# Layer 0's results in DRAM by quarter, line and position, in a two-layer scan of convolutions

## The chip, the cores and the metric

The kernel runs on one core of one Trainium2 chip. The metric is the device time of one execution in microseconds (us), as a median of several runs. A profile is one further execution with the hardware profiler on; its span runs from the first to the last instruction.

## What is computed

The input x is 32 images of 48 channels, 64 rows (H) and 128 columns (W), float32. There are two layers. Each one normalizes its input over groups of channels, runs four scans over it, and adds the result to its input:

```
def step(w, b):
    def f(carry, inp):
        nxt = inp + _conv1d(carry, w, b)        # 5 taps along the line, 48 -> 48 channels
        return (nxt, nxt)
D = scan(down) over h = 1..63;   U = scan(down's weights) over h = 62..0
R = scan(right) over w = 1..127; L = scan(left) over w = 126..0

x = x + _L0_conv_ref(_gn(x), L0 weights)
x = x + _L1_conv_ref(_gn(x), L1 weights)
```

Each line of a scan (a row of 128 positions, or a column of 64) needs the line before it. A row scan of one group of images is 2 x 63 = 126 steps, a column scan 2 x 127 = 254.

## The kernel before

**Work and order.** The 32 images are four groups of 8. Rows are scanned a group at a time, columns a pair of groups at a time, so there are twelve phases, in the fixed order of `PHASES` (L103): rows of layer 0 groups 0 and 1, columns of layer 0 pair 0, rows of layer 0 group 2, rows of layer 1 group 0, rows of layer 0 group 3, columns of layer 0 pair 1, rows of layer 1 groups 1, 2 and 3, columns of layer 1 pairs 0 and 1. They are counted from 0 here, so phase 3 is the rows of layer 0 group 2, phase 7 the rows of layer 1 group 1, phases 10 and 11 the columns of layer 1. That makes 8 x 126 + 4 x 254 = 2024 steps, each of nine matmuls (L856) and three DVE additions out of PSUM (L865), in one chain.

**Tiles.** Eight positions of a line times 48 channels are 384 lines of partitions, that is three tiles (`o` = 0, 1, 2) of 128 partitions. Position `e` (0 to 7) takes the partitions that `PIECES` (L50) gives: 48 channels at a stretch, two of the positions cut in two, so that a tile consists of three or four pieces of 48, 32 or 16 partitions. In a row phase the free axis of a tile runs over h, and over 16 blocks of 8 positions with 8 images each. In a column phase it is turned round: partitions are h modulo 8 and channel, and the free axis goes over w.

**The transposition is in DRAM.** All tensors between phases lie in DRAM: `xin` (the input, reordered), `ups` (`upa`, `upb`: the results of the row scans) and `mid` (layer 0's results, which are layer 1's input). A column phase works on quarters of W (`j` = 0 to 3) in three slots of the arena. A quarter is 2 groups x 3 tiles = 6 units; a unit is 128 partitions x 2048 elements, 1.05 MB. `mid` before is `kept("mid")` (L188): for each group 48 channels, each with 65,536 elements in the order of `by_col` (L243), and a pad.

**Who uses mid.**
- `keep_result` (L790) writes a unit of layer 0's column phases (2 and 6) to `mid`, in pieces of 48, 32 or 16 partitions, each partition one run of 8 KB. It is issued on SP's queue, four steps after `add_residual` (L785, POOL) has added the layer's input to the unit.
- `move_rows` (L657) loads rows for a row phase, in the same pieces; each run is 128 bytes. For layer 1 (phases 4, 7, 8, 9) it reads `mid` through `by_row` (L220), 8 rows a DMA, on SP's queue. `scale_rows` (L680, ACT) normalizes 16 rows in 24 ACTIVATEs after that.
- `load_residual` (L776) loads the unit that is added to a result. In layer 1 (phases 10 and 11) it reads `mid` by `by_col`, in pieces, on ACT's queue; in layer 0 it reads `xin` on SP's.

**The order of the work** is written out: `at(t, fn, ...)` puts a piece of work at step t of the whole chain, and `in_order` (L255) fixes the order of the instructions on every engine and queue as they are traced, so that a queue's next DMA is never issued before the one ahead of it. All DMAs are recorded under L249. The DMAs of SP and ACT take eight semaphores in turn, so that one waits until the DMA eight places before it has landed. `plan_rows` (L968) loads rows 16 at a time (`LOAD`): after a column phase at steps -28, -12, 4 and 20 of the phase, scaled at -13, 3, 19 and 35; otherwise at -54, -43, 0 and 11, scaled at -22, -8, 16 and 30. `plan_cols` (L1011) adds the results of quarters 3, 2, 1, 0, 32 steps from one to the next, a unit each 4.5 steps (7 in quarter 0 ahead of a row phase). In layer 1 a result is then brought into the output's order (`permute_unit`, L806, line L813) and stored (`store_result`, L821, runs of 128 bytes), or held in DRAM (`hold_result`) and sent out later (`let_result`, L834). The last quarter of the last phase is added by DVE after the last step (`last_results`, L1105).

**Statistics.** `scaling` (L352) turns means and variances into scale and offset for a group. In its short form (`if not slack`, L394), used for three groups of x, a variance is spread over partitions by three small matmuls (`expand`, L371), DVE adds a constant, ACT takes the square root (L405), and then the mean is spread (L406).

Of the kernel before, what the change touches and what calls it, by code (L numbers as in the profile page):

```python
# [29 lines left out]
F32 = mybir.dt.float32  # L30
# [3 lines left out]
C = 48  # L34
# [8 lines left out]
E8 = 8  # L43
FULL = 128
NG = E8 * C // FULL
NQ = 4
# [73 lines left out]
def kernel(  # L120
# [67 lines left out]
    def kept(name):  # L188

        return [  # L190
            dram.tile([C, CHANNEL + PAD], F32, tag=f"{name}{g}", name=f"{name}{g}")[:, 0:CHANNEL]
            for g in range(NGRP)
        ]
# [3 lines left out]
            dram.tile([E8 * NQ, C, UNIT], F32, tag=f"xin{g}", name=f"xin{g}")  # L197
            for g in range(NGRP)
        ],
        kept("mid"),  # L200
    ]
    ups = [kept("upa"), kept("upb")]
    taps = [
# [28 lines left out]
    def x_by_col(t, e, j):  # L232


        return t[e * NQ + j]

    def x_put(t, r):

# [4 lines left out]
    def by_col(t, e, j):  # L243


        return t.rearrange("c (i q n) -> i q c n", i=E8, q=NQ)[e, j]

    def dma(dst, src, queue=None):
        (queue or nc.sync).dma_start(dst, src)  # L249
# [34 lines left out]
    def pieces(o):  # L284
        return [(e, c0, c1, p0) for e, c0, c1, g, p0 in PIECES if g == o]
# [66 lines left out]
    def scaling(key, layer, g, averages, masks, slack=0):  # L352


        n = len(masks)
        yield from averages(key, slack)
        mean_p, var_p = averages.result
        pool = nc.gpsimd

        def average(ps, *terms):  # L360
            for k, rhs in enumerate(terms):
                for i in range(n):
                    nc.tensor.matmul(
                        ps,
                        masks[i],
                        rhs[:, i],
                        start=k == 0 and i == 0,
                        stop=k == len(terms) - 1 and i == n - 1,
                    )

        def expand(ps, *terms):  # L371
            for o in range(NG):
                for k, rhs in enumerate(terms):
                    nc.tensor.matmul(
                        ps[:, o], maskp[:, o], rhs, start=k == 0, stop=k == len(terms) - 1
                    )

        def small(name):
            return stat_tile([FULL, NG, GB], name, key)

        ps = ps_stat.tile([FULL, 2 * NG + 2, GB], F32, tag="ps_stat", name=f"ps_{key}")
        average(ps[:, 0], mean_p)
        yield
        scale, offset = (
            stat_pool.tile(
                [FULL, NG, GB], F32, tag=f"{t}{layer}{g}", name=f"{t}{layer}{g}"
            )
            for t in ("scale", "offset")
        )
        coeffs[layer, g] = scale, offset  # L390
        mean, var = ps[:, 1 : 1 + NG], ps[:, 2 + NG :]
        spare = small("dev")
        dev = spare[:, 0:n]
        if not slack:  # L394
            far = ps[:, 1 + NG : 2 + NG]
            nc.vector.tensor_tensor(far, mean_p, ps[:, 0:1], ALU.subtract)
            nc.vector.tensor_tensor(dev, mean_p, ps[:, 0:1], ALU.subtract)
            nc.vector.tensor_tensor(far, far, dev, ALU.mult)
            nc.vector.tensor_tensor(dev, far, var_p, ALU.add)
            yield  # L400
            expand(var, dev[:, 0])
            yield
            nc.vector.tensor_scalar(var, var, GN_EPS, None, ALU.add)
            r0 = small("std")
            nc.scalar.activation(r0, var, AF.Sqrt)  # L405
            expand(mean, mean_p[:, 0])  # L406
            yield
            yield
            nc.vector.reciprocal(r0, r0)
            nc.vector.tensor_tensor(var, var, r0, ALU.mult)  # L410
            nc.vector.tensor_tensor(var, var, r0, ALU.mult)
            nc.vector.tensor_scalar(var, var, -0.5, 1.5, ALU.mult, ALU.add)
            nc.vector.tensor_tensor(scale, var, r0, ALU.mult)
            nc.vector.tensor_tensor(offset, mean, scale, ALU.mult)
            nc.vector.tensor_scalar(offset, offset, -1.0, None, ALU.mult)
            return
        mean_s = small("mean")
        if n > 1:
            mean_c = stat_tile([FULL, GB], "mean_c", key)
            nc.vector.tensor_copy(mean_c, ps[:, 0])  # L420
            yield
            expand(mean, mean_c)
            yield
            nc.vector.tensor_tensor(dev, mean_p, mean, ALU.subtract)
            nc.vector.tensor_copy(mean_s, mean)
        else:
            nc.vector.tensor_tensor(dev, mean_p, ps[:, 0:1], ALU.subtract)
        pool.tensor_tensor(dev, dev, dev, ALU.mult)
        if n == 1:
            pool.tensor_tensor(dev, dev, var_p, ALU.add)  # L430
        yield
        for _ in range(slack):
            yield
        if n == 1:
            expand(var, dev[:, 0])
        else:
            average(ps[:, 1 + NG], dev, var_p)
            yield
            var_c = stat_tile([FULL, GB], "var_c", key)
            nc.vector.tensor_copy(var_c, ps[:, 1 + NG])  # L440
            yield
            expand(var, var_c)
        yield
        var_s = small("var")
        nc.vector.tensor_scalar(var_s, var, GN_EPS, None, ALU.add)
        std = small("std")
        nc.scalar.activation(std, var_s, AF.Sqrt)
        if n == 1:
            expand(mean, mean_p[:, 0])
        yield  # L450
        if n == 1:
            nc.vector.tensor_copy(mean_s, mean)
        yield
        for _ in range(slack):
            yield
        r0 = std
        nc.vector.reciprocal(r0, std)
        t0 = spare
        pool.tensor_tensor(t0, var_s, r0, ALU.mult)
        pool.tensor_tensor(t0, t0, r0, ALU.mult)  # L460
        yield
        pool.tensor_scalar(t0, t0, -0.5, 1.5, ALU.mult, ALU.add)
        pool.tensor_tensor(scale, r0, t0, ALU.mult)
        pool.tensor_tensor(offset, mean_s, scale, ALU.mult)
        pool.tensor_scalar(offset, offset, -1.0, None, ALU.mult)
# [185 lines left out]
    def row_views(k):  # L651
        return [slot[i].rearrange("p (o h n) -> p o h n", o=NG, h=HALF) for i in slots(k)]
# [4 lines left out]
    def move_rows(k, h0, h1, to_dram, q=None):  # L657

        _, layer, g = PHASES[k]
        view = row_views(k)[h0 // HALF]  # L660
        t = (ups if to_dram else source)[layer][g]
        for h in range(h0, h1, E8):
            end = min(h1, h + E8)
            for o in range(NG):
                for e, c0, c1, p0 in pieces(o):
                    here = view[p0 : p0 + c1 - c0, o, h % HALF : h % HALF + end - h]
                    if to_dram or layer:
                        there = by_row(t, e, h, end, q)[c0:c1]
                    else:
                        there = x_by_row(t, e, h, end)[c0:c1]  # L670
                    if q is None:
                        here = here.rearrange("p h (q n) -> p (h q) n", q=NQ)
                    else:
                        here = here[:, :, q * RUN : (q + 1) * RUN]
                    if to_dram:
                        dma(there, here)
                    else:
                        dma(here, there)

    def scale_rows(k, h0, h1):  # L680
        _, layer, g = PHASES[k]
# [36 lines left out]
    def quarter(k, j):  # L718
        return slot[slots(k)[j % 3]].rearrange("p (o s n) -> p s o n", s=2, o=NG)
# [56 lines left out]
    def load_residual(k, j, i, nat):  # L776
        _, layer, pair = PHASES[k]
        o, half = UNITS[i]
        t = source[layer][2 * pair + half]
        for e, c0, c1, p0 in pieces(o):  # L780
            here = nat[p0 : p0 + c1 - c0]
            there = (by_col if layer else x_by_col)(t, e, j)[c0:c1]
            dma(here, there, nc.scalar if layer else None)

    def add_residual(k, j, i, nat, eng=nc.gpsimd):  # L785
        o, half = UNITS[i]
# [3 lines left out]
    def keep_result(k, j, i):  # L790
        _, layer, pair = PHASES[k]
        o, half = UNITS[i]
        for e, c0, c1, p0 in pieces(o):
            dma(
                by_col(source[1][2 * pair + half], e, j)[c0:c1],
                quarter(k, j)[p0 : p0 + c1 - c0, half, o],
            )

    def by_image(t):

# [134 lines left out]
    def at(t, fn, *args):  # L935
        agenda.append((t, len(agenda), fn, args))
# [31 lines left out]
    def plan_rows(k, t0, prev):  # L968
# [5 lines left out]
            ahead, scaled = (-54, -43, 0, 11), (-22, -8, 16, 30)  # L974
        if k:
            for i in range(4):
                at(t0 + ahead[i], move_rows, k, i * LOAD, (i + 1) * LOAD, False)
                at(t0 + scaled[i], scale_rows, k, i * LOAD, (i + 1) * LOAD)

        cuts = list(range(0, H + 1, E8))  # L980
# [397 lines left out]
```

## Time and profile before

| | |
|---|---|
| median of 3 runs | 4215.19 us (4209.02 to 4222.83) |
| the profiled execution's own time | 4228.38 us |
| its span | 4226.6 us |
| granted TensorE clock, mean | 0.984 |
| PE busy | 4086.4 us, 97% |
| last step ends (DVE, L865) | 4144.2 us |
| DMA packets | 2,118,431, of them 2,006,416 under 512 B; 680.55 MB |
| SP's queue | 582.07 MB, 69.0% of 16 engines' span |
| ACT's queue | 87.20 MB, 9.7% |

How to read it: busy times are the union of an engine's instructions. A line of waits names who waited for whom, then the total in us, how often, and the longest. A line of a timeline has start, length, engine, line, operation and tiles, and in brackets the idle time before it and what ended it. A line of a window has its length, each engine's busy time with the count of instructions, the granted clock, the share of the 16 DMA engines' time that packets took (packets overlap, so it can pass 1) and the rate in GB/s. Matmuls are pipelined, so a busy PE isn't a PE at its peak. What ended a wait is inferred from semaphores.

### The profile page before, as it was taken

Reading aid. Unit: us, or ns where it says so; the run is one execution under the profiler, and the core shown is the slowest. Engines: PE = TensorE matmul, PEld = TensorE weight load, DVE = VectorE, ACT = ScalarE, POOL = GpSimd, SP = SyncE. Lnnn points to the kernel's source line nnn. Section 1 sums busy time; section 2 is a strip of 40 time slices with the busy share of each in tenths; the row PEclk is TensorE's granted clock in tenths of the full one; section 3 lists DMA queues with packets and bytes.
Section 4 is the critical chain, followed back from the end, with each engine's and each line's share of the span. In section 5 each row is a group of like instructions: output and inputs, shape, how many; then the busy total and the mean of one; then the engine's idle time right before and its main releaser. Section 6 shows DMA issues by size and latency. Waiting matters only on the chain. (4 is left out here: it accounts for less than half of the span.)

```text
span 4226.6 us, 90155 instructions
## 1 busy us (share of the span) xinstructions
PE 4086.4 (97%) x36724; PEld 4055.0 (96%) x36724; DVE 2135.8 (51%) x6501; ACT 1287.5 (30%) x2525; POOL 791.2 (19%) x737
## 2 busy tenths in 40 slices
PE   8999999999999999999999999999999999999992
PEld 6999999999999999989999999999999999999992
DVE  5454444456644454444457654444444444444443
ACT  6844000536874633000016854503000012110122
POOL 3520010334322100010023310000000034410352
PEclk9999999999999999999999999999999999999996
DMA  9987669659979997259419979759188059899999
GB/s 293 236 174 115 110 126 209 216 148 250 208 187 172 199 151 126 41 102 202 84 48 265 203 144 156 114 80 161 32 147 182 1 99 246 236 260 156 177 202 182
DMA packets 2118431, 680.55 MB, mean 161 GB/s; under 512 B 2006416, under 2 KB 2056832, under 8 KB 2079616
## 3 DMA queue, kind: packets, MB, share of 16 engines
q1 hardware_dynamic: 2015504, 582.07, 69.0%
q10 hardware_dynamic: 99952, 87.20, 9.7%
q0 software_dynamic: 2560, 5.51, 0.5%
q8 instruction: 289, 4.73, 0.5%
q14 instruction: 126, 1.03, 0.1%
HBM read 397.77 MB, written 295.14 MB: 164 GB/s over the span
## 5 line engine op out<-in xcount | busy, mean ns | idle before, releaser
L688 ACT ACTIVATE arena<-arena,offset,scale 128x256 f32<-128x256 f32 (+2 forms) x840 | 582.3, 788 | 310.4 <-DMA arena<-mid 176.8
L788 POOL TENSOR_TENSOR arena<-arena 128x2048 f32<-128x2048 f32 x80 | 362.9, 4548 | 1442.6 <-PE step_10l L856 461.4
L637 POOL COPY arena<-arena 128x256 f32<-128x256 f32 x332 | 196.7, 660 | 443.1 <-DMA arena<-in_x 394.2
L575 ACT ACTIVATE early<-arena 128x256 f32<-128x256 f32 x192 | 129.5, 674 | 453.6 <-DMA arena<-xin 315.2
L856 PE MATMUL step_01r<-arena,early 128*128 128x128 f32 x2286 | 254.2, 275 | 10.0 <-DMA arena<-arena 5.4
L856 PEld LDWEIGHTS step_01r<-arena,early 128*128 128x128 f32 x2286 | 253.3, 187 | 10.9 <-DVE arena L865 6.0
L856 PE MATMUL step_00r<-arena,early 128*128 128x128 f32 x2286 | 253.5, 275 | 8.7 <-DMA arena<-arena 4.4
L856 PEld LDWEIGHTS step_00r<-arena,early 128*128 128x128 f32 x2286 | 252.8, 186 | 9.4 <-issue 4.8
L856 PE MATMUL step_11r<-arena,early 128*128 128x128 f32 x2286 | 251.5, 274 | 5.5 <-DVE arena L865 5.5
L856 PEld LDWEIGHTS step_11r<-arena,early 128*128 128x128 f32 x2286 | 251.0, 185 | 5.9 <-DVE arena L865 5.8
L856 PE MATMUL step_00l<-arena,wleft 128*128 128x128 f32 x2286 | 249.3, 272 | 0.0
L856 PE MATMUL step_01l<-arena,wleft 128*128 128x128 f32 x2286 | 248.7, 272 | 0.1
L856 PEld LDWEIGHTS step_00l<-arena,wleft 128*128 128x128 f32 x2286 | 248.7, 184 | 0.0
L856 PEld LDWEIGHTS step_01l<-arena,wleft 128*128 128x128 f32 x2286 | 248.4, 184 | 0.3 <-DVE arena L865 0.3
L856 PE MATMUL step_10l<-arena,wleft 128*128 128x128 f32 x2286 | 248.5, 272 | 0.0
L856 PE MATMUL step_10r<-arena,early 128*128 128x128 f32 x2286 | 248.5, 272 | 0.0
L856 PE MATMUL step_11l<-arena,wleft 128*128 128x128 f32 x2286 | 248.5, 272 | 0.0
L856 PEld LDWEIGHTS step_10l<-arena,wleft 128*128 128x128 f32 x2286 | 248.4, 184 | 0.0
L856 PEld LDWEIGHTS step_10r<-arena,early 128*128 128x128 f32 x2286 | 248.4, 184 | 0.0
L856 PEld LDWEIGHTS step_11l<-arena,wleft 128*128 128x128 f32 x2286 | 248.4, 184 | 0.0
L813 ACT COPY arena<-arena 128x256 f32<-128x256 f32 x172 | 99.5, 655 | 409.0 <-POOL arena L788 154.1
L260 ACT COPY early<-arena 128x1 f32<-128x1 f32 x2 | 0.4, 192 | 655.0 <-DVE arena L865 655.0
(200 smaller groups left out, 7090.7 us busy)
## 6 DMA issues: line engine op xcount, KB each, us to landing
xin<-arena SPq DMA_DIRECT2D x91, 512.0 KB, 4.2
arena<-in_x SPq DMA_DIRECT2D x18, 2048.0 KB, 11.0
arena<-xin SPq DMA_DIRECT2D x96, 384.0 KB, 8.7
mid<-arena SPq DMA_DIRECT2D x96, 384.0 KB, 8.1
arena<-mid SPq DMA_DIRECT2D x192, 192.0 KB, 4.3
upb<-arena SPq DMA_DIRECT2D x192, 192.0 KB, 3.9
arena<-upb SPq DMA_DIRECT2D x96, 384.0 KB, 12.4
arena<-xin SPq DMA_DIRECT2D x180, 192.0 KB, 4.3
```

The lines of the kernel that those rows point to most:

```text
L260: fn(*args)
L575: nc.scalar.activation(junk[:, 0:n], view[:, b], AF.Identity, accum_out=self.sum[:, i, j : j + 1])
L637: copy(dst[:, r, q], src[:, r0 + r, q])
L688: nc.scalar.activation(args[0], args[0], AF.Identity, bias=args[2], scale=args[1])
L788: eng.tensor_tensor(unit, unit, nat, ALU.add)
L813: copy(by_w(perm)[:, a], src[:, a])
L856: nc.tensor.matmul(part(whole(ps[o])[0:m], -s), weights[:, i, at : at + m], part(src(i), s), start=seen[o] == 1, stop=seen[o] == left[o],)
```

## The change

`mid` becomes, for each group, four quarters x 8 lines x 384 (position and channel) x 256 elements. A unit's eight lines are then 1 KB runs, and 128 neighbouring partitions are neighbours in DRAM. `by_unit` names a unit there as one transfer of 128 partitions; the third tile, whose pieces are not in order, takes two, of 96 and of 32. `keep_result` and layer 1's `load_residual` use it. Layer 1's rows are loaded by `take_rows`, which takes one tile `o` of 16 rows at a time, a quarter of W in a DMA; the three tiles are placed 2 steps before, 1 step after and 4 steps after the time that `move_rows` had. Apart from that, the mean's `expand` in `scaling` is traced right after that of the variance.

```diff
--- before.py
+++ after.py
@@ -197,7 +197,10 @@
             dram.tile([E8 * NQ, C, UNIT], F32, tag=f"xin{g}", name=f"xin{g}")
             for g in range(NGRP)
         ],
-        kept("mid"),
+        [
+            dram.tile([NQ, NH, E8 * C, LINE], F32, tag=f"mid{g}", name=f"mid{g}")
+            for g in range(NGRP)
+        ],
     ]
     ups = [kept("upa"), kept("upb")]
     taps = [
@@ -233,6 +236,25 @@
 
 
         return t[e * NQ + j]
+
+    def by_quarter(t, e, h0, h1, q):
+
+
+        t = t[q].rearrange("a (i c) (e n) -> e c (a i) n", i=E8, e=E8)
+        return t[e, :, h0:h1]
+
+    def by_unit(t, o, j):
+
+
+        at = [(o * FULL, 0, FULL)]
+        if o == NG - 1:
+            at = [(6 * C, 0, 2 * C), (5 * C + C // 3, 2 * C, FULL)]
+        t = t[j].rearrange("a m n -> m a n")
+        return [(t[r : r + p1 - p0], p0, p1) for r, p0, p1 in at]
+
+    def by_line(t):
+
+        return t.rearrange("p (a n) -> p a n", a=NH)
 
     def x_put(t, r):
 
@@ -399,11 +421,11 @@
             nc.vector.tensor_tensor(dev, far, var_p, ALU.add)
             yield
             expand(var, dev[:, 0])
+            expand(mean, mean_p[:, 0])
             yield
             nc.vector.tensor_scalar(var, var, GN_EPS, None, ALU.add)
             r0 = small("std")
             nc.scalar.activation(r0, var, AF.Sqrt)
-            expand(mean, mean_p[:, 0])
             yield
             yield
             nc.vector.reciprocal(r0, r0)
@@ -664,7 +686,7 @@
             for o in range(NG):
                 for e, c0, c1, p0 in pieces(o):
                     here = view[p0 : p0 + c1 - c0, o, h % HALF : h % HALF + end - h]
-                    if to_dram or layer:
+                    if to_dram:
                         there = by_row(t, e, h, end, q)[c0:c1]
                     else:
                         there = x_by_row(t, e, h, end)[c0:c1]
@@ -676,6 +698,18 @@
                         dma(there, here)
                     else:
                         dma(here, there)
+
+    def take_rows(k, h0, h1, o):
+
+        _, layer, g = PHASES[k]
+        view = row_views(k)[h0 // HALF]
+        for e, c0, c1, p0 in pieces(o):
+            here = view[p0 : p0 + c1 - c0, o, h0 % HALF : h0 % HALF + h1 - h0]
+            for q in range(NQ):
+                dma(
+                    here[:, :, q * RUN : (q + 1) * RUN],
+                    by_quarter(source[layer][g], e, h0, h1, q)[c0:c1],
+                )
 
     def scale_rows(k, h0, h1):
         _, layer, g = PHASES[k]
@@ -777,10 +811,12 @@
         _, layer, pair = PHASES[k]
         o, half = UNITS[i]
         t = source[layer][2 * pair + half]
-        for e, c0, c1, p0 in pieces(o):
-            here = nat[p0 : p0 + c1 - c0]
-            there = (by_col if layer else x_by_col)(t, e, j)[c0:c1]
-            dma(here, there, nc.scalar if layer else None)
+        if layer:
+            for there, p0, p1 in by_unit(t, o, j):
+                dma(by_line(nat)[p0:p1], there, nc.scalar)
+        else:
+            for e, c0, c1, p0 in pieces(o):
+                dma(nat[p0 : p0 + c1 - c0], x_by_col(t, e, j)[c0:c1])
 
     def add_residual(k, j, i, nat, eng=nc.gpsimd):
         o, half = UNITS[i]
@@ -790,11 +826,8 @@
     def keep_result(k, j, i):
         _, layer, pair = PHASES[k]
         o, half = UNITS[i]
-        for e, c0, c1, p0 in pieces(o):
-            dma(
-                by_col(source[1][2 * pair + half], e, j)[c0:c1],
-                quarter(k, j)[p0 : p0 + c1 - c0, half, o],
-            )
+        for there, p0, p1 in by_unit(source[1][2 * pair + half], o, j):
+            dma(there, by_line(quarter(k, j)[:, half, o])[p0:p1])
 
     def by_image(t):
 
@@ -974,7 +1007,12 @@
             ahead, scaled = (-54, -43, 0, 11), (-22, -8, 16, 30)
         if k:
             for i in range(4):
-                at(t0 + ahead[i], move_rows, k, i * LOAD, (i + 1) * LOAD, False)
+                if PHASES[k][1]:
+                    for o in range(NG):
+                        t = t0 + ahead[i] - 2 + 3 * o
+                        at(t, take_rows, k, i * LOAD, (i + 1) * LOAD, o)
+                else:
+                    at(t0 + ahead[i], move_rows, k, i * LOAD, (i + 1) * LOAD, False)
                 at(t0 + scaled[i], scale_rows, k, i * LOAD, (i + 1) * LOAD)
 
         cuts = list(range(0, H + 1, E8))
```

## Prediction

> **What bounds the kernel now.** I read the page first, then PE's waits, then the time per step (three DVE results end a step, 2024 steps), then windows around each stall and after the last step, then ACT's, POOL's and DVE's timelines there.
>
> ```profile
> PE 4086.4 (97%) x36724; PEld 4055.0 (96%) x36724; DVE 2135.8 (51%) x6501; ACT 1287.5 (30%) x2525; POOL 791.2 (19%) x737
> DMA  9987669659979997259419979759188059899999
> ```
>
> PE is the bound while it runs: each step needs the one before it, and takes 1.975 us in a row phase and 1.955 us in a column phase (medians of the DVE ends). The last step ends at 4144.2 us. So two things can be shortened: PE's stalls, and the 82 us from there to 4226.6. The stalls, by time over the median step: first group until 116 us, 19; seams into phases 2 and 6, some 14 and 16; phase 3 (layer 0 rows, at 1098) 10.9 at rows 32 and 2 at each of the two steps at row 48, so 14.8; phase 7 (layer 1 rows, at 2383) 6.6 at row 48; phase 11 (at 3640) 8.1 at column 64. The waits of PE, whole run:
>
> ```profile
> PE step_02d L856 <- issue: 8.2, 3, 6.5
> PE step_11r L856 <- DVE arena L865: 5.5, 1, 5.5
> ...
> PE step_11d L856 <- DVE arena L865: 3.6, 1, 3.6
> ...
> PE ps_x L374 <- ACT std_x L405: 2.2, 3, 0.8
> ```
>
> The releaser named is the last semaphore only; ACT's waits show what was late. For row 48 of phase 7 (window 2440 to 2486) and row 32 of phase 3 (1136 to 1205):
>
> ```profile
> ACT arena L688 <- DMA arena<-mid: 5.2, 2, 3.1
> ```
> ```profile
> ACT arena L688 <- DMA arena<-xin: 16.3, 4, 7.4
> ```
>
> So the scaling (24 ACTIVATEs) starts late because the row load landed late, and SP's timeline shows why: its queue runs without a gap, L790's writes to mid and L776's loads between the row loads. After the last step DVE adds the residual of quarter 0 and waits for each:
>
> ```profile
> 4157.17 2.29 DVE L788 TENSOR_TENSOR arena<-arena 128x2048 f32<-128x2048 f32 x1 [3.27 <-DMA arena<-mid]
> ...
> 4168.45 2.29 DVE L788 TENSOR_TENSOR arena<-arena 128x2048 f32<-128x2048 f32 x1 [7.25 <-DMA arena<-mid]
> ...
> 4178.99 2.29 DVE L788 TENSOR_TENSOR arena<-arena 128x2048 f32<-128x2048 f32 x1 [6.50 <-DMA arena<-mid]
> ...
> 4189.06 2.29 DVE L788 TENSOR_TENSOR arena<-arena 128x2048 f32<-128x2048 f32 x1 [6.03 <-DMA arena<-mid]
> ```
>
> Stages by window (columns: length, busy PE, PEld, DVE, ACT, POOL with counts, clock, DMA share, GB/s):
>
> ```profile
> 52.00:58.00 6.00, 6.00 (x8) 2.15 (x7) 6.00 (x12) 6.00 (x14) 5.83 (x10) 1.00 1.09 385
> 864.00:884.00 20.00, 20.00 (x187) 20.00 (x186) 9.61 (x30) 0.00 (x0) 0.00 (x0) 1.00 0.97 170
> 938.00:958.00 20.00, 20.00 (x187) 20.00 (x186) 14.56 (x42) 15.35 (x38) 13.59 (x5) 1.00 0.76 183
> 3405.00:3429.00 24.00, 24.00 (x223) 24.00 (x222) 11.97 (x38) 0.00 (x0) 0.00 (x0) 1.00 1.01 202
> 1187.00:1197.00 10.00, 10.00 (x93) 10.00 (x92) 6.97 (x20) 9.18 (x13) 0.00 (x0) 1.00 0.90 225
> 3700.00:3704.00 4.00, 4.00 (x37) 3.83 (x36) 1.92 (x6) 0.00 (x0) 0.00 (x0) 1.00 1.03 424
> 3810.00:3900.00 90.00, 90.00 (x832) 90.00 (x831) 44.26 (x138) 0.00 (x0) 0.00 (x0) 1.00 1.06 157
> 3965.00:4226.00 261.00, 178.79 (x1646) 178.59 (x1645) 113.20 (x294) 59.84 (x104) 123.60 (x86) 0.85 1.22 194
> ```
>
> These are the prices. A unit is 1.05 MB. Read in pieces of 48, 32 or 16 partitions it moves at 170 (xin, 864) or 202 GB/s (mid, 3405), that is 6.2 or 5.2 us; written to mid in such pieces at 225 (1187), 4.7 us. Whole 128-partition transfers move at 424 with 8 KB runs (spill, 3700; 2.5 us) and at 385 with 1 KB runs (xin<-arena, 52; 2.7 us). Results leave in 128-byte runs at 157 (3810), 6.7 us a unit.
>
> **What the Trainium skill says.** "SBUF — State Buffer", Door 1: a DMA is as fast as the number of the 16 SBUF ports that its partitions reach, and partitions 0 to 63 reach eight of them. The trace agrees: 170 to 225 GB/s in pieces, 385 to 424 whole. "DMA: Bandwidth & Descriptors", Why small descriptors are slow: a fixed overhead per packet; here 385 at 1 KB against 424 at 8 KB, 10%. The same page, Queues, rings and completion order: an engine takes packets from its queues in turn; no run here separates this, and I use it only for a rival. "TensorE: Matmul & The Clock Gate", Part 1: after an idle window of about 3.4 us the clock halves; the trace agrees, the clock is 0.50 for 10.2 us after the stall at 1160 and 6.8 us after that at 3764, so a stall costs its wait and some 2 to 3 us more.
>
> **The change, part by part.**
>
> *Writes of layer 0's results (keep_result, 48 units, SP):* 160 DMAs become 64, 4.7 us becomes 2.7. In mixture with xin loads the packets did not reach their lone rate, so I take 1.1 us a unit (ends: 0 and 2). Between 1010, where SP last waited for POOL, and the end of the row load at 1150, SP issued 31 pieces, 9.3 units: 10 us less ahead of rows 32 to 47. Then they land at about 1142 in place of 1156, scaling of 19 us ends at 1161, and the row is needed at 1160. Late next is ACT itself: its statistics (13.5) and the scaling of rows 48 to 63 (19 to 23) follow without a gap and end at about 1194, for a need at 1192. Of 14.8 us I take 10 (0 to 14.8). Phase 7: 12 units or so lie in the full queue from 2300 on; the load of rows 48 to 63 need come only 5.2 us earlier, then ACT ends at 2476 for a need at 2476.5. I take 5 (0 to 6.6).
>
> *Row loads of layer 1 (take_rows, SP, four phases):* each 16 rows become 40 DMAs in place of 20, 640 for 320 in all; runs are 128 bytes as before, the same number. An issue on SP takes at least 0.30 us (the shortest of mid), 40 make 12 us; the data take 26 us now (20 DMAs, 2398.8 to 2425.1), so issuing is covered, unless the data were twice as fast. The three parts of a load are put 2 steps before, 1 and 4 after the old time, on SP alone. In phase 7 the instruction list of the changed kernel puts the last part of rows 32 to 47 behind a residual load and L790's first unit of quarter 0, and two parts of rows 48 to 63 behind that of the third unit, which waits for POOL's add: about 3 us, taken off above. The parts also pass the writes of the last phase's rows to upb, which wait 0.2 to 0.9 us each for DVE: nothing beside the slack. Phases 4, 8 and 9 have no stall for rows: in phase 8 rows 32 to 47 are issued at step 0 and needed at 32, while load (11 steps) and scaling (10) take 21. The new address order, 48 KB from run to run where 8 and 32 KB stood, is shown nowhere; xin, read with 384 KB and more between runs, costs the same as mid: 40 DMAs, two loads, took SP 43 us from xin (1565 to 1608) and 40 from mid (2595 to 2635), 13 to 14 ns for each of a load's 1536 packets an engine. I take 0 (ends: minus 2 us; or 14 ns doubled, the last rival).
>
> *Residuals of layer 1 (load_residual, 48 units, ACT's queue):* 160 DMAs become 64, 5.2 us becomes 2.7. No row shows a read in 1 KB runs; xin's writes in such runs are the nearest, and in_x is read in 2 KB runs at 403 GB/s (window 800 to 804). Ends: 2.6 and 5.2 us; I take 2.7. In phase 10 POOL's adds of quarter 0 started at 3665 to 3750 where the plan (8.8 us apart from 3646) has the last start at 3690, each waiting for mid. With 2.5 us less for each of 24 units this lag is gone by 3700, and some 13 MB of mid and held no longer lie beside phase 11's loads of upb for column 64: they have 3715 to 3764 for 6 units at 5 to 6 us. Of 8.1 us I take 7.
>
> *The end:* from 3965 to 4226 went 24 stores (160 us at 157), 18 residuals (94) and 6 spill units (15): 269 us of transfers in 261, so DMA sets the end. With 2.7 they make 224. But results come only every 8.8 us, six in each 32 steps (62.6). Work per unit 9.4, in the first quarter 12; behind by 19 − 10 after the first, 3 after the second, 7 when the third is out, with its last store some 6 more: 13 us at 4144. Then six stores, 40, and 2 for landing: 55 in place of 82. I take 26 (0 to 36; the floor is the add, the copies and six stores).
>
> *Expansion of the mean before the square root (L406 moved):* no instruction more; PE no longer waits for ACT in three places, 2.2 us. DVE's add on var follows three small matmuls later, 0.3 each. I take 2 (1 to 3).
>
> Sum: 10 + 5 + 0 + 7 + 26 + 2 = 50. The profiled execution took 4228.4 (span 4226.6), so 4178 for it; it lay 13.2 above the median of the runs, 4215.2, and the waits are the same work in both: **4165**.
>
> **Rivals.** (a) Reads in 1 KB runs stay at 5 us, because of DRAM or because packets of two queues alternate and a 1 KB run gets an eighth of the turn. Phase 11 and the end keep their times: gain 17, 4198. Against it: in_x. (b) Only the reads gain; the mixture of xin pieces and mid is bound by xin, so rows stay late: 7 + 26 + 2, 4180. (c) Everything goes, all stalls and 35 of the end: 67, 4148. (d) Slower: row loads at 48 KB stride take 28 ns a packet. A load then takes 43 us, 22 steps; phases 4, 8 and 9 miss row 48 by 6 steps (12 us each), phase 7 by 28 us and phase 3 gains; 36 + 28 + 10 of clock against the 45 of phase 3, phase 11, the end and L406: 4244. It decides from about 22 ns, where the slack of 6 steps (12 us over 1536 packets an engine) is used up. (e) It does not do what it says to the time: the transfers are cheaper, but whatever is freed is taken by the queue's next entries, and only L406 and 1 us stay: 4212.
>
> **How the numbers follow.** Forecast 0.55, (a) 0.14, (b) 0.12, (c) 0.07, (d) 0.08, (e) 0.04. The range leaves out (d) and (e) and half of (c): 4148 to 4202. A measurement of this kernel can tell about 0.3% from no change, 13 us. Faster 0.88, same 0.04, slower 0.08.
>
> **What would show it.** Right: no PE wait at column 64 of phase 11, mid loads alone near 385 GB/s, DVE's adds after the last step without 6 us waits, a tail near 55 us. Wrong: packets of 128 bytes from mid over 20 ns, ACT L688 waiting longer for mid in phases 4, 8 and 9, a tail still near 80.

## The result, and the profile after

The changed kernel takes 4201.56 us (median of 12 runs, 4190.4 to 4211.33), the kernel before 4220.92 (12 runs): a ratio of 0.9956, 95% interval 0.9944 to 0.9968. That is 19 us less, where 50 were forecast. The profiled execution took 4201.03 us (span 4199.2), 27.4 less than that of before, which lay 7.5 above its own median.

The page after, engines and the 40 slices of DMA, then its packets:

```profile
PE 4083.1 (97%) x36724; PEld 4050.4 (96%) x36724; DVE 2133.5 (51%) x6501; ACT 1287.7 (31%) x2525; POOL 787.0 (19%) x737
...
DMA  9987669669969999258419968948379019999799
...
DMA packets 2206497, 680.57 MB, mean 162 GB/s; under 512 B 2008465, under 2 KB 2157185, under 8 KB 2179969
```

The bytes are the same. 100,353 more packets are under 2 KB: units of mid go in 1 KB runs (98,304 packets). Busy times say nothing of the gain; PE's waits do (all of the run, the largest):

```profile
PE step_00d L889 <- DVE arena L898: 11.8, 7, 6.4
PE step_11d L889 <- issue: 9.4, 1, 9.4
PE step_02d L889 <- issue: 9.3, 2, 8.6
PE step_11d L889 <- DVE arena L898: 8.9, 3, 8.0
```

`step_11r` waiting for DVE (5.5 us before, at column 64 of phase 11) is gone, and so is `ps_x` waiting for ACT. `step_11d`, the rows of phase 7, waited 4.8 on these two and now waits 18.3. After the last step, DVE's adds of the last quarter:

```profile
4143.90 2.28 DVE L824 TENSOR_TENSOR arena<-arena 128x2048 f32<-128x2048 f32 x1
...
4152.22 2.73 DVE L824 TENSOR_TENSOR arena<-arena 128x2048 f32<-128x2048 f32 x1
...
4165.39 2.73 DVE L824 TENSOR_TENSOR arena<-arena 128x2048 f32<-128x2048 f32 x1
```

None waits for mid, where four waited 3 to 7 us. The last is out at 4168 instead of 4191. Windows of the changed kernel (columns as before: the clock, the DMA share and GB/s stand last):

```profile
3965.00:4199.00 234.00, 178.59 (x1644) 178.40 (x1642) 113.01 (x294) 59.84 (x104) 119.36 (x86) 0.89 1.24 216
4144.00:4199.00 55.00, 0.00 (x0) 0.00 (x0) 24.74 (x18) 13.20 (x23) 12.71 (x18) 0.52 1.31 174
3412.00:3424.00 12.00, 12.00 (x113) 12.00 (x112) 5.76 (x18) 0.00 (x0) 0.00 (x0) 1.00 1.05 334
```

The same work moves at 216 GB/s, 194 before. Residuals alone ran at 334, where the window from 3405 before, which holds residuals alone too, had 202. That is 3.1 us a unit. The tail is full to its end (share 1.31), so that transfers still set it is the likely reading.

Where the time went, as time over the median step (1.975 us in a row phase, 1.955 in a column phase), and from the last step to the end of the span (the tail), in us. All phases are counted without their first step, which in phases 2 and 6 took another 6.5 to 8.7 us over the median in every kernel of the table:

| kernel | phase 2 | phase 3 | phase 6 | phase 7, its first step in brackets | phase 11 | tail | span |
|---|---|---|---|---|---|---|---|
| before | 9.5 | 21.5 | 9.8 | 13.6 (0.1) | 8.6 | 82.4 | 4226.6 |
| after | 4.8 | 22.1 | 2.2 | 32.3 (0.3) | 0.8 | 55.2 | 4199.2 |
| residuals in pieces | 4.8 | 20.9 | 2.2 | 34.9 (0.3) | 10.5 | 81.7 | 4239.1 |
| results kept in pieces | 5.2 | 23.4 | 8.9 | 37.0 (0.3) | 0.8 | 57.4 | 4217.1 |
| before, rows 4 a DMA | 4.8 | 22.3 | 7.3 | 25.3 (0.1) | 6.6 | 77.2 | 4227.5 |
| old times | 4.4 | 22.8 | 2.5 | 29.9 (0.3) | 0.8 | 54.6 | 4198.4 |
| GpSimd, all loads | 4.6 | 20.6 | 2.8 | 12.3 (8.9) | 0.7 | 55.0 | 4190.4 |
| GpSimd, rows 32 to 63 | 11.6 | 20.8 | 2.7 | 17.5 (0.6) | 0.7 | 56.1 | 4191.3 |
| that, loads earlier | 10.7 | 21.6 | 8.8 | 23.5 (0.6) | 0.7 | 55.6 | 4203.3 |
| that, phase 3 too | 9.6 | 17.0 | 8.8 | 23.9 (0.6) | 0.7 | 54.7 | 4198.1 |
| that, writes to mid too | 9.9 | 25.8 | 2.1 | 23.3 (0.3) | 0.8 | 55.7 | 4199.7 |
| mean's expansion back | 4.8 | 18.5 | 2.2 | 31.6 (0.3) | 0.8 | 55.8 | 4198.6 |

("That" is the version with rows 32 to 63 on GpSimd's queue.) What differs in phases 2 and 6 lies at their starts. The start of phase 2 is the same code in most of these kernels and still spreads from 4.4 to 11.6; a difference of 7 us there or at the start of phase 6 is therefore not read as an effect. Phase 7 of three kernels with rows 32 to 63 on GpSimd's queue at the same steps gave 17.5, 23.9 and 23.3; the changed kernel and two with the same writes and row loads gave 32.3, 34.9 and 31.6 there, and 22.1, 20.9 and 18.5 in phase 3. So 3 us in phase 7 and 4 in phase 3 aren't read as an effect either.

So phase 11 and the tail gave 35 us, and phase 7 took 19 back.

### The profile page after: what moved, and what is told of

Same layout as the page of the kernel before. It is cut to its first block, busy times and chain, and to the rows that moved or that the text cites. A ratio compares the mean times of both kernels' runs of the same rounds, so it can differ in the third digit from the quotient of the medians.

```text
span 4199.2 us, 90284 instructions
## 1 busy us (share of the span) xinstructions
PE 4083.1 (97%) x36724; PEld 4050.4 (96%) x36724; DVE 2133.5 (51%) x6501; ACT 1287.7 (31%) x2525; POOL 787.0 (19%) x737
```

## The experiments

**Residuals of layer 1 in pieces again**, everything else as after:

```diff
-            for there, p0, p1 in by_unit(t, o, j):
-                dma(by_line(nat)[p0:p1], there, nc.scalar)
+            for e, c0, c1, p0 in pieces(o):
+                dma(by_line(nat)[p0 : p0 + c1 - c0], by_piece(t, e, j)[c0:c1], nc.scalar)
...
+    def by_piece(t, e, j):
+        return t[j].rearrange("a (i c) n -> i c a n", i=E8)[e]
```

> The changed kernel, with layer 1's residuals loaded from the new layout in the old pieces of 48, 32 and 16 partitions. If whole 128-partition transfers are what shortened the end and took away the stall at column 64 of phase 11, both come back: a tail of about 80 us in place of 55, 5 to 8 us at column 64, time about 4232. If it was the new order in DRAM (1 KB runs next to each other) and not the partitions, nothing comes back: 4202.

4243.53 us, a ratio to before of 1.0046 (1.003 to 1.0062). Tail 81.7, phase 11 10.5. DVE's adds after the last step:

```profile
4168.64 2.29 DVE L827 TENSOR_TENSOR arena<-arena 128x2048 f32<-128x2048 f32 x1 [3.30 <-DMA arena<-mid]
4179.74 2.29 DVE L827 TENSOR_TENSOR arena<-arena 128x2048 f32<-128x2048 f32 x1 [7.08 <-DMA arena<-mid]
4190.54 2.29 DVE L827 TENSOR_TENSOR arena<-arena 128x2048 f32<-128x2048 f32 x1 [6.77 <-DMA arena<-mid]
4201.18 2.29 DVE L827 TENSOR_TENSOR arena<-arena 128x2048 f32<-128x2048 f32 x1 [6.60 <-DMA arena<-mid]
```

and PE's wait of phase 11:

```profile
PE step_11r L892 <- DVE arena L901: 7.7, 1, 7.7
```

The waits of before are back, and the adds are some 10.8 us apart again. A window with residuals alone:

```profile
3418.00:3430.00 12.00, 12.00 (x113) 12.00 (x112) 5.77 (x18) 0.00 (x0) 0.00 (x0) 1.00 1.13 193
```

The runs have 1 KB in both forms, 193 GB/s here and 334 in the changed kernel, so it is the pieces of 48, 32 and 16 partitions against 128, and not the length of the run. Nor is it the issue of the 160 DMAs on ACT's queue: the transfers are full (share 1.13). The tail came as expected, phase 11 and the time somewhat above. This one part of the change is worth some 37 us (10 in phase 11, 27 in the tail), nearly twice what the whole change brings.

**The kernel before, with its layer 1 rows loaded 4 at a time**: 40 DMAs for 16 rows in place of 20, the same bytes, runs and addresses, nothing else of the change.

```diff
-        for h in range(h0, h1, E8):
-            end = min(h1, h + E8)
+        by = E8 // 2 if layer and not to_dram else E8
+        for h in range(h0, h1, by):
+            end = min(h1, h + by)
```

> The kernel before, with layer 1's rows loaded 4 at a time in place of 8: 40 DMAs for 16 rows as in the changed kernel, the same bytes and runs, the old layout, times and order. Theory A (issue): phase 7's 13.6 us over its steps grow to 28 to 38, time 15 to 20 us above before. Theory B (placement): no difference from before, within 5 us.

4233.88 us, 1.0016 (1.0003 to 1.0028): slower than before by some 7 us. Phase 7 went from 13.6 to 25.3 by the number of DMAs alone, a little under the 28 to 38 that the first theory had. Two loads in a row in phase 8 show why. SP's timeline (start, length, queue, tiles, count) of before, of this kernel, and of the changed kernel:

```profile
2594.98 40.40 SPq L249 DMA_DIRECT2D arena<-mid  x40
```
```profile
2611.15 48.12 SPq L249 DMA_DIRECT2D arena<-mid  x80
```
```profile
2603.48 51.01 SPq L271 DMA_DIRECT2D arena<-mid  x80
```

and windows inside these stretches, in the same order:

```profile
2597.00:2634.00 37.00, 37.00 (x340) 37.00 (x339) 18.12 (x57) 37.00 (x51) 1.42 (x6) 1.00 1.08 156
```
```profile
2613.00:2657.00 44.00, 44.00 (x404) 44.00 (x403) 21.40 (x67) 38.68 (x52) 1.41 (x6) 1.00 0.83 132
```
```profile
2605.00:2652.00 47.00, 47.00 (x429) 46.91 (x428) 22.89 (x72) 45.72 (x62) 1.42 (x6) 1.00 0.82 127
```

With 40 DMAs the transfers are full (share 1.08), and SP's instructions are long; that they wait to be taken is the reading. With 80 the transfers are not full (0.83 and 0.82) while SP issues without a gap. It doesn't wait for landings there either (in the changed kernel 1.1 us in two waits, both for PE). So it is SP's issuing that is the bound. In phase 7 itself the share during the load of rows 32 to 47 fell from 1.09 (2399 to 2425) to 0.83 (2404 to 2433) by the number alone. The DMAs in those stretches, before and after (shortest, median, longest in ns):

```profile
L249 SPq DMA_DIRECT2D arena<-mid x40: 432/894/2606, 2595.0 to 2634.0; - x40
```
```profile
L271 SPq DMA_DIRECT2D arena<-mid x80: 303/527/2072, 2603.5 to 2654.0; - x80
```

The shortest, 303 ns, is what the prediction took for every one. The usual issue takes 527 ns for 48 partitions, 487 for 32 and 447 for 16, and 44 to the next. Of ten pieces six have 48 partitions, two 32 and two 16, so that is 547 ns a DMA: 80 make 44 us, and 47 to 51 were seen.

**Old times**: the three tiles of a load at one step, as `move_rows` had them, instead of 2 before, 1 and 4 after.

```diff
-                        t = t0 + ahead[i] - 2 + 3 * o
-                        at(t, take_rows, k, i * LOAD, (i + 1) * LOAD, o)
+                        at(t0 + ahead[i], take_rows, k, i * LOAD, (i + 1) * LOAD, o)
```

> The changed kernel, with the three tiles of a row load of layer 1 placed together at the time that the kernel before had, in place of 2 steps before, 1 and 4 after. Theory A (issue): phase 7's new stalls at rows 16 and 32 come from 40 DMAs whose issue takes SP about 0.57 us each, 27 to 32 us for 16 rows where 20 DMAs took 25; then placement matters little, phase 7 keeps 20 to 30 us over its steps, time 4195 to 4205. Theory B (placement): the last part of a load stands behind a residual load and a unit's write; then the stalls at rows 16 and 32 go, phase 7 is at 12 us or less over its steps, time about 4182.

4197.73 us, 0.9931 (0.9916 to 0.9945). Phase 7: 29.9 for 32.3. The placement explains 2 of phase 7's 19, if that.

**The middle tile's 16 DMAs of a row load on GpSimd's queue**, on top of the old times, so that SP issues 24:

```diff
                     by_quarter(source[layer][g], e, h0, h1, q)[c0:c1],
+                    nc.gpsimd if o == 1 else None,
```

> The changed kernel with row loads at the old times (as the run with old times), and the middle tile's 16 of 40 DMAs of each load of layer 1's rows issued by GpSimd. If SP's issue is what makes a load long, SP has 24 DMAs of 0.57 us, 14 us, and the data's 21 set the time again: phase 7's loads take 22 to 27 us, its excess over its steps falls from 30 to 10 to 15 us, time about 4182. If the new address order or the DMA engines are the limit, it stays at 28 to 32 and 4198. Risk on the other side: GpSimd's adds wait behind these issues and the time rises above 4205.

4192.32 us, 0.993 (0.9911 to 0.9949). Two loads in a row of phase 8, and a window in them:

```profile
2587.46 36.59 SPq L271 DMA_DIRECT2D arena<-mid  x48
```
```profile
2589.00:2624.00 35.00, 35.00 (x322) 35.00 (x321) 17.14 (x54) 34.98 (x48) 13.39 (x25) 1.00 1.05 148
```

36.6 us instead of 51.0, and the transfers are full again (1.05): two queues issue what one could not. Phase 7 fell from 29.9 to 12.3, as expected, but the risk that was named came too: its first step now waits 8.9. GpSimd's and ACT's timelines ahead of it show why:

```profile
2314.92 9.13 POOL L271 DMA_DIRECT2D arena<-mid  x14
2325.19 0.56 POOL L271 DMA_DIRECT2D arena<-mid  x1 [1.13 <-DMA arena<-mid]
2328.18 0.56 POOL L271 DMA_DIRECT2D arena<-mid  x1 [2.43 <-DMA arena<-xin]
2328.75 13.57 POOL L825 TENSOR_TENSOR arena<-arena 128x2048 f32<-128x2048 f32 x3
```
```profile
2333.33 0.68 ACT L597 ACTIVATE early<-arena 128x256 f32<-128x256 f32 x1 [34.95 <-POOL arena L825]
...
2360.79 17.99 ACT L723 ACTIVATE arena<-arena,offset,scale 128x256 f32<-128x256 f32 x24
```

GpSimd's adds stand behind 14 us in which it issues, or waits to issue, its row DMAs; ACT's statistics, which come ahead of the scaling in ACT's order, wait 35 us for an add, 21 in the changed kernel; the scaling of rows 0 to 15 begins at 2360.8, against 2344.3 in the changed kernel, whose phase 6 ended 3 us earlier.

**GpSimd's queue for rows 32 to 63 only**, which leaves those adds alone:

```diff
+                    nc.gpsimd if o == 1 and h0 >= 2 * LOAD else None,
```

> The changed kernel with the three tiles of a layer 1 row load at one step, and the middle tile's 16 DMAs on GpSimd's queue, but only for rows 32 to 63 of a phase; rows 0 to 31 stay on SP, so that ahead of phase 7 no add on GpSimd stands behind DMAs of rows. Theory (SP's in-order queue with some 0.57 us of issue for each of 40 DMAs is what makes rows late in phase 7): the excess of phase 7 is near 12 us as with GpSimd for all loads (32 in the changed kernel), and the wait at its first step is back at 2 instead of 9, so about 4185 us, 0.8 to 0.9% under the kernel before. Rival (phase 7 gained there only because it began 9 us late, which gave its loads 9 us): the excess is 20 to 25 with the first step at 2, about 4192 to 4197, no better than before this edit.

4192.64 us, 0.9932 (0.9915 to 0.9948). The first step is back at 0.6 and phase 7 at 17.5; both theories had a number that it misses. Two of the kernels below have the same loads there and gave 23.9 and 23.3, so the rival is nearer: with the first step counted in, GpSimd for all loads gave 21.2 and this form 18.1 to 24.5. About half of what phase 7 gained in the run before came from beginning later.

**The same with earlier loads**, and **the same with phase 3's rows 32 to 63 split between the queues too**:

```diff
-            ahead, scaled = (-28, -12, 4, 20), (-13, 3, 19, 35)
+            ahead, scaled = (-28, -14, 3, 15), (-13, 3, 19, 35)
```

> As the run before it, with the row loads after a column phase at steps -14, 3 and 15 in place of -12, 4 and 20 (layer 0's phase 3 too); the slots are free from step 2 on, after the last statistics of quarter 1, and no residual load is passed by more than 5 steps of row loading. Theory: row 48 has its data 5 steps, 10 us, earlier, so the stalls at row 48 go, phase 3's by 2 to 5 us of 22 and phase 7's by 2; row 32 gains 1 step; about 4178 to 4183. Rival (what is freed is taken by what stands behind: the residuals of quarter 0 and the units kept come later, and with them the statistics that set when layer 1's coefficients are there): no gain or a loss of up to 5 us, and new waits after step 50 of phases 3 and 7.

4193.39 us, 0.9939 (0.9916 to 0.9961): nothing gained, phase 3 21.6, phase 7 23.5, as the rival had it.

```diff
-                        dma(here, there)
+                        dma(here, there, nc.gpsimd if k == 3 and o == 1 and h0 >= 2 * LOAD else None)
```

> Where phase 3's expected 10 us are. On top of the version with GpSimd's queue for the middle tile of rows 32 to 63 of layer 1: the same for rows 32 to 63 of phase 3, which are 40 DMAs from xin, 20 for 8 rows. Theory (phase 3 is held by SP's in-order queue like phase 7; its load of rows 32 to 47 occupies SP for 31 us): the excess of phase 3 goes from 21 to 10 to 14, about 4184 us. Rival (its loads are bound by the transfers themselves, whose share is 1.0 to 1.1 in the 20 us ahead of them, and the writes to mid never held them): it stays at 19 to 22 and the time at 4192.

4196.69 us, 0.9936 (0.991 to 0.9961). Phase 3 went from 20.8 to 17.0, a difference that its spread would allow; but the stall at row 48, which every other kernel of the table has, is gone, and that at row 32 stays, between the two theories. PE's wait for row 32, and two windows ahead of it:

```profile
PE step_02d L890 <- issue: 6.8, 1, 6.8
```
```profile
1100.00:1120.00 20.00, 20.00 (x185) 20.00 (x184) 11.98 (x36) 16.31 (x27) 11.86 (x10) 1.00 1.07 228
1120.00:1140.00 20.00, 20.00 (x185) 20.00 (x184) 11.91 (x35) 18.69 (x41) 15.31 (x10) 1.00 1.03 213
```

A share of 1.03 to 1.07 with two queues issuing: row 32 of phase 3 waits for transfers rather than for SP.

**Results kept in pieces again**, and **the writes to mid on GpSimd's queue**, two ways to ask what `keep_result` is worth:

```diff
-        for there, p0, p1 in by_unit(source[1][2 * pair + half], o, j):
-            dma(there, by_line(quarter(k, j)[:, half, o])[p0:p1])
+        t = source[1][2 * pair + half]
+        for e, c0, c1, p0 in pieces(o):
+            dma(by_piece(t, e, j)[c0:c1], by_line(quarter(k, j)[p0 : p0 + c1 - c0, half, o]))
```

> The changed kernel, with layer 0's results written to the new layout in the old pieces. The prediction had 1.1 us a unit gained by whole transfers, 10 us ahead of row 32 of phase 3: if so, the stall there grows by 8 to 10 us and phase 7's too, time 4215 or more. If the mixture with xin's pieces sets the rate (rival b), nothing changes: phase 3 at 20 to 24 us over its steps as after, time 4198 to 4206.

4219.23 us, 0.9983 (0.9976 to 0.9991). Set against the changed kernel's ratio, whole units are worth 0.27% or 11 us, some 6 either way. The time came as the first theory had it, phase 3 (23.4 for 22.1) as the rival. Phase 7 shows 37.0 where kernels with whole units and the same row loads gave 31.6 to 34.9, so 2 to 5 of it; another 6.7 are at the start of phase 6. In the table all three kernels with pieces began that phase at 7.3 to 9.8 and seven of nine with whole units at 2.1 to 2.8, but two at 8.8. No DMA of mid is issued between 1700 and 2000 in the profile of before or after, so that part is likely chance.

```diff
-            dma(there, by_line(quarter(k, j)[:, half, o])[p0:p1])
+            dma(there, by_line(quarter(k, j)[:, half, o])[p0:p1], nc.gpsimd)
```

> On the same base, the writes of layer 0's results to mid are issued on GpSimd's queue, after its adds, so that none of them stands in SP's queue ahead of the row loads of phases 3 and 7. Theory of the prediction (these writes, as entries of SP's queue, hold the rows up): phase 3 goes from 21 to 12 or less and phase 7 from 17 to 12, about 4180 us. Rival (the writes cost the rows nothing by their place; what is ahead of the rows is the xin pieces, which take the transfers): phases 3 and 7 within 3 us of what they were, about 4192; where GpSimd's adds come later by the issue of two DMAs each, up to 4200.

On the version with GpSimd's queue for rows 32 to 63: 4201.46 us, 0.9954 (0.9935 to 0.9973). Phase 3 went up from 20.8 to 25.8, with a new stall at row 16, phase 7 is in its spread. Taking the writes to mid out of SP's queue altogether brought the rows no earlier. The place of these writes ahead of the rows is not what holds phase 3.

**Row loads much earlier**, first with SP alone, then with GpSimd's queue for the middle tile:

```diff
-            ahead, scaled = (-28, -12, 4, 20), (-13, 3, 19, 35)
+            ahead, scaled = (-34, -22, -1, 12), (-13, 3, 19, 35)
```

> The changed kernel with the row loads after column phases (3 and 7) at steps -34, -22, -1, 12 in place of -28, -12, 4, 20, tiles together. If a load that takes 28 to 35 us of issue is only late, 8 to 10 steps earlier take away the stalls at rows 16 to 48 of phase 7 and most of row 32 of phase 3: phase 7 from 30 to about 8 us, phase 3 from 22 to about 12, time about 4165. If the queue is full of older work whatever the place (DMA bound), the stalls move to other rows and the time stays within 8 us of 4198.

> Both: row loads earlier and the middle tile of layer 1's rows on GpSimd. If issue on SP and place are both causes, the best of these: phase 7 at about 6 us over its steps (only the small matmuls of the statistics), time about 4163. If they are the same cause, no better than the run with earlier loads.

4290.25 us, 1.0168 (1.0152 to 1.0183), and 4290.04, 1.0165 (1.015 to 1.018). The row stalls did go (with SP alone, phase 3 from 22 to 8.8, phase 7 from 30 to 9.0), but phases 2 and 6 lost 24 to 32 us each, and the first steps after them waited another 29 to 42. The first of these waits, on DVE, in the kernel with SP alone:

```profile
1058.67 0.62 DVE L573 BATCH_NORM_STATS2 bn_r<-arena 128x6 f32<-128x256 f32 x1 [23.62 <-DMA arena<-xin]
```

In both kernels the loads come before the last statistics of the quarters whose slots they fill (the ones placed at −34 and −1), so part of the computation is changed: for a few images DVE's statistics read loaded rows in place of layer 0's results. That is where DVE waits, and the scan with it. These two show that a load at −34 or −1 meets a slot still in use; they say nothing of what earlier loads would cost in free slots.

**The mean's expansion back behind the square root**, everything else as after:

```diff
             expand(var, dev[:, 0])
-            expand(mean, mean_p[:, 0])
             yield
...
             nc.scalar.activation(r0, var, AF.Sqrt)
+            expand(mean, mean_p[:, 0])
```

> The changed kernel with the mean's small matmuls traced after the square root as before. The prediction gave this part 2 us: the waits of PE for ACT (0.5, 0.8, 0.8 us) come back and nothing else; phases 0, 2 to 7 as in the changed kernel otherwise. It is also a second profile of all the rest: if the start of phase 6 is near 9 us over its steps here, that difference between the kernels is chance.

A single run, 4200.39 us; it can't tell 2 us. PE's waits can:

```profile
PE ps_x L396 <- ACT std_x L427: 2.2, 3, 0.8
```

These 2.2 us, the same as before, are absent from the changed kernel's waits.

## Why the prediction was wrong

It forecast 50 us, and 19 (27 between the profiled executions) came. The step that failed is the price of the row loads: SP's issuing was taken as covered, and it became the bound. By its own terms:

- *The end*, 26: right, 27.2. It left 55 us, as worked out, and the version with residuals in pieces brings 82 back. As a residual took 3.1 us alone and not 2.7, some 7 us more for the 18 of them, that it met 55 so closely is in part luck.
- *Residuals at 2.7 us a unit, and phase 11*, 7: right in phase 11, 7.8, with a unit at 3.1 us. That version brings 10 back. So rival (a), reads in 1 KB runs that stay slow, is refuted. "SBUF — State Buffer", Door 1, in the Trainium skill, on which this step rested, agrees: 1 KB runs on 128 partitions gave 334 GB/s and no waits, the same runs on 16 to 48 gave 193 and the waits of before. Not all of POOL's late adds in phase 10 were shown as waiting for mid, as the prediction read them: of the six from 3665 on, the line of the first names PE and that at 3720 no releaser.
- *L406*, 2: right in what can be seen, 2.2 of PE's waits.
- *keep_result in phase 7*, 5: a size near it was found (2 to 5), though it doesn't show, as the row loads took some four times as much there.
- *keep_result ahead of rows 32 to 63 of phase 3*, 10: wrong, 21.5 became 22.1. The step was "1.1 us a unit" for 9.3 units in SP's queue. The units did get cheaper to issue, but the load of rows 32 to 47 was issued from 22 us after the phase's start in both kernels and had landed 54 us after it before and 56 after, and without any such write in SP's queue phase 3 did not get better. What lies ahead of these rows are pieces from xin, which the change leaves as they are; transfers there are near full (share 0.81 to 1.12 in stretches of 10 us from 1100 to 1150, both kernels). Rival (b) had this one right.
- *Row loads*, 0: this is the step that failed. "An issue on SP takes at least 0.30 us (the shortest of mid), 40 make 12 us; the data take 26 us now, so issuing is covered": the shortest of 320 was taken as the price of each. The usual one and the gap to the next are 0.55 us, so 40 make 22 us. The 26 us that it was set against held more than the data: its longest DMA stood on SP for 6.5 us, with three pieces of a unit queued just ahead of it. The data alone need 20, which 22 exceed. A load took SP 19.7 to 21.0 us in phases 8 and 9 and takes 23.0 to 25.7. There it is hidden, as said. In phase 7, where rows had no slack, the load of rows 32 to 47 landed at 2427.8 before and at 2438.0 after, although the phase's first step ended 12.6 us earlier (2371.2 for 2383.8). SP's issues of it and ACT's scaling, before:

```profile
2398.76 26.34 SPq L249 DMA_DIRECT2D arena<-mid  x20
```
```profile
2427.88 16.55 ACT L688 ACTIVATE arena<-arena,offset,scale 128x256 f32<-128x256 f32 x22 [1.92 <-PE step_11d L856]
```

And after, with PE's stall:

```profile
2397.93 21.96 SPq L271 DMA_DIRECT2D arena<-mid  x28
...
2421.90 13.16 SPq L271 DMA_DIRECT2D arena<-mid  x12
```
```profile
2438.12 16.40 ACT L722 ACTIVATE arena<-arena,offset,scale 128x256 f32<-128x256 f32 x22 [13.46 <-PE step_11d L889]
```
```profile
2453.54 0.77 PE L889 MATMUL step_11d<-arena,early 128*128 128x128 f32 x2 [9.38 <-issue]
```

The releaser that is named, PE, is the last semaphore only; the landing at 2438.0 tells what it waited for.

What this step cost in phase 7 is some 21 to 24 us: 18.7 that show and the 2 to 5 of whole writes that it hides. Four kernels tell how it came about. The table has, for the four loads of 16 rows of phase 7, the time of their DMAs on SP (with 44 ns after each), and when they had landed, in us from the phase's start:

| kernel | SP's time | landed |
|---|---|---|
| before | 23.0, 24.5, 24.0, 25.7 | -44.8, 3.6, 46.1, 83.0 |
| before, rows 4 a DMA | 26.3, 28.8, 27.5, 27.4 | -39.5, 12.2, 58.9, 96.1 |
| old times | 28.4, 32.5, 29.9, 34.5 | -39.3, 13.6, 59.6, 98.7 |
| after | 35.8, 44.0, 35.1, 32.3 | -29.6, 24.1, 69.1, 103.0 |

The number of DMAs alone adds 2 to 4 us of SP to each load. The delays add up in its queue, so that rows 32 to 47 land 13 us later, and phase 7 shows 11.7. The three times of a load, the last of them 4 steps (8 us) after the old one, add another 10 of landing, where the prediction had 3; of that phase 7 shows only 2.4, as its stalls are then at rows 16 and 32 and not at 32 and 48. The remaining 5, between the old times and the kernel before with rows 4 a DMA (29.9 for 25.3), are less than the spread of 6 between kernels with the same loads and stay open. The first load is issued 70 to 71 us ahead of the phase in all four, so that the phase began earlier isn't what made its rows late.

Rival (d) had the place right, row loads that become the bound, and the mechanism wrong: a packet of 128 bytes took 13 ns in the median in both address orders (the mean was 13.1 in the new one and 14.1 in the old, in the two windows of phase 8), so 48 KB from run to run cost nothing. Of what the prediction named as signs, the wait at column 64, the adds and the tail came as it said, and mid alone ran at 334 GB/s, not near 385. Of the signs of being wrong one came: ACT's waits for mid grew around phase 4 (7.1 to 14.3 us), phase 8 (131 to 159) and phase 9 (0 to 6.9), though these phases themselves lost no more than 1 us each. It was phase 7, which the prediction didn't name there, that paid.

Between the profiles, the end (27.2), phase 11 (7.8) and the first group (2.4) came as said; phase 7 lost 18.8, phase 3 0.5 and phases 8 and 9 1.4; and 10.5 came at phases 2 and 6, first steps counted, which no step foresaw and which the spread there allows as chance: 27.2, for 27.4 measured. The medians, 19 apart, hold less of that chance.

The versions that issue rows from two queues, 4192.32 and 4192.64 us, are the fastest measured, 0.7% under the kernel before. Their intervals overlap with that of the changed kernel, so that they beat it is likely and not shown.

## What to carry to other kernels

Cutting a transfer so that it fills 128 partitions pays on the side that is cut, but look at what the new layout does to everyone else who reads it: here one reader got fewer and wider transfers, and another got twice as many. Count a queue's DMAs by the median issue of that shape, not by the shortest, and compare with what the data take alone. Here a DMA share of 0.82 to 0.85 in a stretch of back-to-back issues told that the issuing engine was the bound, where 1.05 and more went with full transfers. A second queue then helped at once (two loads in 36.6 us for 51.0), but its engine's own work stood behind the issues.

## What the runs showed of the hardware

- An issue on SP took 447, 487 and 527 ns in the median for 16, 32 and 48 partitions of 16 runs of 128 bytes in the changed kernel, and 44 ns to the next. In the kernel before with rows 4 a DMA, whose runs are 4 by 4, it took 526 or 527 for all three. A load of 3.15 MB in 40 DMAs is 79 KB each, at 0.547 us at most 144 GB/s from one queue; 127 to 132 were seen. "DMA: Bandwidth & Descriptors" in the Trainium skill, Issuing engines are not separate DMA queues, calls the time to initiate a DMA usually small relative to the DMA itself; here it was the larger, and splitting the issues between SP and GpSimd took two loads from 51.0 us to 36.6.
- How long a DMA instruction stood on SP depended on the transfers, and not on its size alone: 894 ns in the median before, at a share of 1.08, and 527 after, at 0.82, with half the data in each.
- A residual read alone in pieces ran at 202 GB/s with runs of 8 KB (before) and at 193 with runs of 1 KB: in pieces the shorter runs cost little. Filling 128 partitions with the runs of 1 KB gave 334. A packet of 1 KB took 91 ns in the median in pieces and 48 on 128 partitions, in these windows.
